# A convolution-attention kernel: layer 1's side projections on two column groups of TensorE, placed behind the sums over the values, and sums of weights used one and a half steps later

## The chip, the cores and the metric

The kernel runs on one core of one Trainium2 chip. The metric is the device time of one execution in microseconds (us), the median of three runs. Everything is computed in fp32.

## The reference

The input is x, two images of 256 channels and 64 x 64 = 4096 positions. Two attention layers follow each other; the second works on the output of the first.

```
layer 0: xn = layernorm over channels(x);  q, k, v = qkv_w xn    (4 heads of 16)
         attn = softmax(q k^T / 4) * gate(x);  x1 = sigmoid(gamma * out_w(attn v) + x)
layer 1: q, k, v = w_qkv x1 + b_qkv                             (4 heads of 64)
         attn = softmax(q k^T / 8) over 4096 positions
         out = w_out(attn v) + b_out + x1
```

The change touches layer 1 alone. There each image has 4 heads of 64 channels, and each head a 4096 x 4096 matrix of scores.

## The kernel before

**How layer 1 is tiled.** Two heads are worked on together: head 0 of a pair on partitions 0 to 63, head 1 on 64 to 127. A *unit* is (image, pair, block of 512 queries): 2 x 2 x 8 = 32 units, one after the other. Within a unit the keys come in 32 chunks of 128. A *step* takes two chunks, so a unit has 16 steps, and the 512 steps run as one long pipeline. In a step, the first chunk is called chunk 0 and the second chunk 1.

For each chunk the following is done:

- score (L876, TensorE): keys times queries, both heads at once on two row groups (64x128 tiles), into a pair of PSUM banks. There are two such pairs, one for each chunk of a step (in the first unit's beginning a third helps).
- keep (L893 and L894): VectorE takes the running maximum rmax over the chunks from the banks; then ScalarE copies the scores to SBUF (raw). The second copy frees the banks.
- 22 chunks (LAG = 11 steps) later, when the maximum of the group of 16 chunks is known: shift (L951, VectorE) adds the negated maximum, weigh (L963, ScalarE) takes the exponential in place, and GpSimd adds the result to a running sum of weights acc (L973 for the first two of a group, then L975).
- gather (L1004, TensorE): values times weights, summed over the 16 chunks of a group in one bank (av), the two heads on two column groups (128x64 tiles). At the end of a group ScalarE copies av out (L1015).

**The order is written out by hand.** Every instruction is kept in program order on its engine (seq). A main loop runs over the steps t and issues, besides the chunk work, whatever was hung at (t, place) by at():

```
scores = [score(c) for c in pair] if inside else []
weigh(pair[1] - 2 * LAG - 2)         # the exponential of the step before
hung(t, "start"); hung(t, "early")
keep(pair[0], scores[0]); shift(pair[0] - 2 * LAG); weigh(pair[0] - 2 * LAG)
hung(t, "early end")
keep(pair[1], scores[1])
for c in pair: gather(c - 2 * LAG - 2)
hung(t, "late"); hung(t, "late end")
shift(pair[1] - 2 * LAG); hung(t, "end")
```

(The loop is shortened; conditions for the first and last steps are left out.) So TensorE's order in a step is: scores of both chunks, what is hung at early, the sums over the values of two chunks, what is hung at late. ScalarE's order is: exponential of the step before, what is hung at start, first copy, exponential, what is hung at early end, second copy.

**What is hung there.** Beside the chunk work, each unit computes things for later units. Counted in steps from the unit's first:

- Keys for the next pair or image: the projection in quarters in steps 2 to 5 (next_keys, quarter, L806), one matmul of 128 channels x 256 positions a step; then store_keys (L818, ScalarE, step 5), and a DMA to DRAM (kd).
- Values: four blocks of 128 positions, each with two matmuls, one block in each of steps 6, 7, 9 and 10 (next_values, values_in, L693); store_values (L832) in steps 7 and 10, the DMA (vd) behind the second.
- Queries of the next unit: quarters in steps 11 (two), 13 and 14 (next_queries); keep_next_queries (L858) in steps 11 and 14. Their input is fetched on SyncE's queue (L656) into three rotating buffers, which the keys' and values' input shares.
- In the last eight units there are no keys and values to make. In their places the first image's output is projected (project_out, L1160) and evacuated (output, L1170).
- The maxima of each group of 16 chunks: turn_max (rt, L906, four transposes) in steps 0 and 8, once early and once late; fold (L923, VectorE, negs), a round trip through DRAM (L926, L930), and place_shift (L943, ScalarE) at the end of steps 2 and 10.
- The sums of weights of the unit before: total (L1026, eight passes on four column groups of 32) in step 12 early; keep_total (L1034, and L1046 for the factor lost) in step 12, with four DMAs to DRAM (L1039) and one back (L1041); add_sums on GpSimd (L1117, L1118) in step 13, late end; factors in step 15, start: the reciprocal on VectorE (L1124) and a product on GpSimd (L1125).
- The output rows of the unit before that: turn_sums (turned, L1051) in step 1, early and late; rows (L1135 on VectorE, L1141 and L1144 on GpSimd), then the store att (L1149).

All small results (k1p, v1p, q1p, o, rt, sum, turned) pass through one PSUM bank (misc, psm with bufs=1): the next one can start only when the one before has been evacuated.

Of the kernel before, what the change touches and what calls it, by code (L numbers as in the profile page):

```python
# [14 lines left out]
P = 128  # L15
NB = 512
C = 256
CC = C // P
H = 4
D0 = 16  # L20
D1 = 64
# [5 lines left out]
def conv_attention_kernel(  # L27
# [19 lines left out]
    nc = tc.nc  # L47
# [78 lines left out]
    for s in range(3):  # L126
        t = const_prep.tile([P, CC, P], F32, tag=f"wpad{s}", name=f"wpad{s}")
# [80 lines left out]
    seq = tc.keep_in_program_order  # L208
# [3 lines left out]
    def at(t, place, step):  # L212
        extras.setdefault((t, place), []).append(step)
# [19 lines left out]
    with own0:  # L233
# [456 lines left out]
        def values_in(ps, xt, g, k):  # L690

            for c in range(CC):
                seq(nc.tensor.matmul(  # L693
                    ps[:, bass.ts(k, P)], xt[:, c, bass.ts(k, P)], w1[:, c, 2, bass.ts(g, P)],
                    start=(c == 0), stop=(c == CC - 1),
                ))
# [71 lines left out]
    with (  # L768
# [31 lines left out]

        def quarter(ps, xt, g, t, q):

            c, cols = q % 2, bass.ts(q // 2, NB // 2)
            seq(nc.tensor.matmul(  # L806
                ps[:, cols], w1[:, c, t, bass.ts(g, P)], xt[:, c, cols],
                start=(c == 0), stop=(c == CC - 1),
            ))

        def next_keys(b, g, i, q):
            if q == 0:
                halves_of["k"] = misc(f"k1p_{b}_{g}_{i}")
            quarter(halves_of["k"], loaded["kv", b, g, i], g, 1, q)

        def store_keys(b, g, i):
            k = l1.tile([P, NB], F32, tag="kv", name=f"k1s_{b}_{g}_{i}")
            seq(nc.scalar.activation(  # L818
                k, halves_of.pop("k"), AF.Identity, bias=b1[:, g, 1:2]
            ))  # L820
            nc.sync.dma_start(out=kd[b, g, i], in_=k)

        def next_values(b, g, i, q):
            if q % 2 == 0:
                halves_of["vp"] = misc(f"v1p_{b}_{g}_{i}_{q}")
            values_in(halves_of["vp"], loaded["kv", b, g, i], g, q)

        def store_values(b, g, i, half):
            if half == 0:
                halves_of["v"] = l1.tile([P, NB], F32, tag="kv", name=f"v1s_{b}_{g}_{i}")  # L830
            v, cols = halves_of["v"], bass.ts(half, NB // 2)
            seq(nc.scalar.copy(v[:, cols], halves_of.pop("vp")[:, cols]))  # L832
            if half == 1:
                loaded.pop(("kv", b, g, i))
                nc.sync.dma_start(out=vd[b, g, i], in_=v)
# [11 lines left out]
        def next_queries(u, q):  # L847
            b, g, j = u
            if q == 0:
                qt = l1x.tile([P, NB], F32, tag="q", name=f"q1_{b}_{g}_{j}")  # L850
                qs1[u] = qt
            if q % 2 == 0:
                halves_of["q"] = misc(f"q1p_{b}_{g}_{j}_{q}")
            quarter(halves_of["q"], loaded["q", u], g, 0, q)

        def keep_next_queries(u, half):
            cols = bass.ts(half, NB // 2)
            seq(nc.scalar.activation(  # L858
                qs1[u][:, cols], halves_of.pop("q")[:, cols], AF.Identity,
                bias=b1[:, u[1], 0:1],  # L860
            ))
            if half == 1:
                loaded.pop(("q", u))
# [154 lines left out]
        def total(u):  # L1018


            b, g, j = u
            srows[u] = misc(f"sum1_{b}_{g}_{j}")
            for n in range(NG):
                for k in range(2):
                    r = D1 * n + 32 * k
                    seq(nc.tensor.matmul(  # L1026
                        srows[u][r : r + 32, :], ones[:, :32], accs[u, n][:, k, :],
                        start=True, stop=True,
                    ))
# [126 lines left out]
        def project_out(b, j, o, q):  # L1156
            if q == 0 or o == 1 and q == 2:
                outs["ps"] = misc(f"o1_{b}_{j}_{o}_{q}")
            c, cols = q % 2, bass.ts(q // 2, NB // 2)
            seq(nc.tensor.matmul(  # L1160
                outs["ps"][:, cols], wo1[:, c, bass.ts(o, P)], loaded["ao", b, j][:, c, cols],
                start=(c == 0), stop=(c == CC - 1),
            ))

        def output(b, j, o, part):

# [23 lines left out]

        for n, u in enumerate(units):
            b, g, j = u
            t0 = n * US
            if n > 0:
                at(t0 - 9, "start", lambda u=u, b=b, j=j: fetch(("q", u), x1[b][j]))
                for q in range(4):
                    at(t0 - (5, 5, 3, 2)[q], "early", lambda u=u, q=q: next_queries(u, q))
                at(t0 - 5, "early end", lambda u=u: keep_next_queries(u, 0))  # L1200
                at(t0 - 2, "early end", lambda u=u: keep_next_queries(u, 1))
            if n < len(units) - NJ:
                to = (*units[n + NJ][:2], j)
                at(max(t0 - 1, 0), "start", lambda to=to: fetch(("kv", *to), x1[to[0]][to[2]]))
                for q in range(4):
                    at(t0 + 2 + q, "early", lambda to=to, q=q: next_keys(*to, q))
                    at(t0 + (6, 7, 9, 10)[q], "early", lambda to=to, q=q: next_values(*to, q))
                at(t0 + 5, "early end", lambda to=to: store_keys(*to))
                for i, step in enumerate((t0 + 7, t0 + 10)):
                    at(step, "early end", lambda to=to, i=i: store_values(*to, i))  # L1210

                t1 = (n // NJ * NJ + NJ - 1) * US
                at(t1 + 2 * j + 2, "start", lambda to=to: load_keys(*to))
                at(t1 + 2 * j + 3 + LAG, "start", lambda to=to: load_values(*to))
            for k in range(NG):
                t1 = t0 + (k + 1) * GS // 2
                places = ("early", "early" if (u, k) == (units[-1], NG - 1) else "late")
                for i, place in enumerate(places):
                    at(t1, place, lambda u=u, k=k, i=i: turn_max(u, k, i))
                    at(t1, f"{place} end", lambda u=u, k=k, i=i: fold(u, k, i))  # L1220
                at(t1 + 2, "end", lambda u=u, k=k: place_shift(u, k))
            t1 = t0 + US + GS // 2
            if u != units[-1]:
                at(t1 + 4, "early", lambda u=u: total(u))
                at(t1 + 4, "early end", lambda u=u: keep_total(u))
                at(t1 + 1, "late", lambda u=u: lose(u))
                at(t1 + 5, "late end", lambda u=u: add_sums(u))
                at(t1 + 7, "start", lambda u=u: factors(u))
                for place, k in (("early", 1), ("late", 0)):
                    at(t1 + 9, place, lambda u=u, k=k: turn_sums(u, k))  # L1230
                    at(t1 + 9, f"{place} end", lambda u=u, k=k: rows(u, k))
            else:
                at(END + 1, "late", lambda u=u: last_lost(u))
                at(END + 4, "early", lambda u=u: late_sums((None, None)))
                at(END + 4, "early end", lambda u=u: keep_late(0))
                at(END + 5, "early", lambda u=u: turn_late(0))
                at(END + 5, "early end", lambda u=u: add_late(u, 0))
                at(END + 6, "early", lambda u=u: turn_sums(u, 0))
                at(END + 6, "early end", lambda u=u: first_rows(u))
                at(END + LAG, "late", lambda u=u: turn_late(1))  # L1240
                at(END + LAG, "late", lambda u=u: add_late(u, 1))
                at(END + LAG, "late", lambda u=u: turn_sums(u, 1))
                at(END + LAG, "late", lambda u=u: last_rows(u))
            if n >= len(units) - NJ:
                b0 = B - 2
                at(t0 - 1, "start", lambda b0=b0, j=j: fetch_output(b0, j))
                for o in range(CC):
                    for q in range(4):
                        step = t0 + ((2, 3, 4, 5), (6, 7, 9, 10))[o][q]
                        at(step, "early", lambda b0=b0, j=j, o=o, q=q: project_out(b0, j, o, q))  # L1250
                at(t0 + 5, "early end", lambda b0=b0, j=j: output(b0, j, 0, 2))
                for part, step in enumerate((t0 + 7, t0 + 10)):
                    at(step, "early end", lambda b0=b0, j=j, part=part: output(b0, j, 1, part))

# [169 lines left out]
```

## Time and profile before

| what | us |
|---|---|
| three runs: median (lowest to highest) | 4672.76 (4672.19 to 4673.68) |
| profiled execution: its own time | 4667.5 |
| profiled execution: span from first to last instruction | 4665.7 |
| first score matmul of layer 1, from the span's start | 2057.6 |
| from one unit's first score matmul to the next one's (units 10 and 11) | 79.80 |
| busy over the span: TensorE / VectorE / ScalarE / GpSimd | 4496.5 / 3894.2 / 3429.5 / 2513.9 |

How to read it: the profile page gives, per engine, the time in which an instruction was under way. TensorE's figure includes waiting inside its pipeline, so a TensorE that is called busy need not be at its peak. Layer 1 is regular: from the second unit on, units follow each other at 78.7 to 80.5 us, so one unit (here unit 10, 2834.7 to 2914.5 us) stands for all. In the timeline a line is: start in us, length in us, engine, line, operation, output<-inputs, shape, number of instructions merged, and in brackets the idle time ahead of it and what ended it. In the list of waits a line is: who <- whom, total us, times, longest us. VectorE's rows overlap a little: an L951 or L893 row is 1.21 us long, and the next one starts 1.13 us after it.

### The profile page before, as it was taken

To read this page: it belongs to the slowest core of one execution; us is meant where nothing else is said; L and a number is where in the kernel's file an instruction comes from. 1 tells how busy PE (TensorE), PEld (TensorE's weight loads), DVE (VectorE), ACT (ScalarE), POOL (GpSimd) and SP (SyncE) were. 2 spreads that over 40 slices of the span, in tenths; PEclk is the share of its full clock that TensorE was granted. 3 is DMA by queue.
4 is the path that set the end of the run, shared out by engine and by line. 5 is a ranking of instruction groups with operands and counts; after the bars stand their busy time and mean duration, and the time that the engine had idled before them with its cause. 6 is when DMAs were issued, how large, how long until landed. Compare 5 with 4: busy or idle time off the path is not lost. (4 is left out here: it accounts for less than half of the span.)

```text
span 4665.7 us, 70910 instructions
## 1 busy us (share of the span) xinstructions
PE 4496.5 (96%) x27290; PEld 1511.0 (32%) x27290; DVE 3894.2 (83%) x4506; ACT 3429.5 (74%) x4588; POOL 2513.9 (54%) x1306
## 2 busy tenths in 40 slices
PE   8999999999999999999999999999999999999998
PEld 3433333333333333332333333333333333222232
DVE  6777777777777777439999999999999999999997
ACT  3366666666666666668888888888888888888885
POOL 5300000000000000009999999999999999999995
PEclk9999999999999999999999999999999999999999
DMA  3100000000000000121111221111211112121213
GB/s 100 39 4 20 20 20 15 15 15 15 15 17 15 15 13 13 40 77 35 35 37 33 63 48 42 35 37 43 69 41 39 37 33 62 48 53 37 53 39 111
DMA packets 199682, 174.70 MB, mean 37 GB/s; under 512 B 121256, under 2 KB 122088, under 8 KB 199344
## 3 DMA queue, kind: packets, MB, share of 16 engines
q1 hardware_dynamic: 197488, 169.58, 13.9%
q8 instruction: 214, 3.51, 0.3%
q14 instruction: 124, 1.02, 0.1%
q10 hardware_dynamic: 1856, 0.59, 0.1%
HBM read 127.65 MB, written 42.48 MB: 36 GB/s over the span
## 5 line engine op out<-in xcount | busy, mean ns | idle before, releaser
L975 POOL TENSOR_TENSOR acc<-acc,raw 128x1024 f32<-128x1024 f32 x883 | 2095.2, 2373 | 82.3 <-ACT raw L963 21.1
L402 DVE TENSOR_REDUCE mx<-a 128x1 f32<-128x512 f32 x2048 | 1314.4, 685 | 449.7 <-PE a L398 448.7
L439 ACT ACTIVATE p<-s 128x512 f32<-128x512 f32 x2048 | 1107.8, 595 | 702.1 <-PE a L398 369.3
L876 PE MATMUL s<-q,k 64*128 64x512 f32 x4096 | 1120.9, 637 | 126.1 <-ACT raw L894 117.9
L951 DVE TENSOR_TENSOR raw<-raw,shift 128x1024 f32<-128x1024 f32 x1024 | 1234.2, 1209 | 3.9 <-ACT shift L943 2.6
L893 DVE TENSOR_TENSOR rmax<-s,rmax 128x1024 f32<-128x1024 f32 x960 | 1168.7, 1217 | 74.4 <-PE s L876 68.3
L436 PE MATMUL s<-q,kT 32*128 32x512 f32 x4096 | 1218.0, 640 | 0.0
L894 ACT COPY raw<-s 128x1024 f32<-128x1024 f32 x1024 | 1034.2, 1010 | 207.3 <-DVE rmax L893 162.0
L963 ACT ACTIVATE raw<-raw 128x1024 f32<-128x1024 f32 x1024 | 1084.8, 1060 | 133.6 <-DVE raw L951 101.2
L398 PE MATMUL a<-kT,q 32*128 32x512 f32 x4096 | 1129.3, 643 | 1.4 <-DVE mx L402 1.3
L1004 PE MATMUL av<-raw,v 128*64 128x512 f32 x4096 | 992.8, 605 | 3.5 <-ACT raw L963 3.4
L451 PE MATMUL av<-p,v 128*32 128x256 f32 (+1 forms) x7904 | 650.1, 399 | 0.6 <-ACT avs L465 0.6
L876 PEld LDWEIGHTS s<-q,k 64*128 64x128 f32 x4096 | 314.6, 185 | 858.5 <-ACT raw L894 600.9
L501 POOL TENSOR_TENSOR f<-f,dyn 128x16 f32<-128x16 f32 x15 | 3.3, 221 | 1027.3 <-DVE f L500 1027.3
L436 PEld LDWEIGHTS s<-q,kT 32*128 32x128 f32 x4096 | 397.2, 183 | 425.8 <-issue 392.6
L451 PEld LDWEIGHTS av<-p,v 128*32 128x32 f32 x7904 | 157.7, 108 | 751.4 <-issue 737.1
L1004 PEld LDWEIGHTS av<-raw,v 128*64 128x64 f32 x4096 | 247.7, 136 | 468.8 <-issue 350.1
L552 POOL TENSOR_SCALAR res<-res 128x1024 f32<-128x1024 f32 x16 | 16.7, 1045 | 659.6 <-ACT res L551 659.6
L398 PEld LDWEIGHTS a<-kT,q 32*128 32x128 f32 x4096 | 305.1, 183 | 31.5 <-DVE mx L402 18.2
L973 POOL TENSOR_TENSOR acc<-raw,raw 128x1024 f32<-128x1024 f32 x64 | 152.6, 2385 | 124.2 <-ACT raw L963 124.2
L923 DVE TENSOR_REDUCE negs<-rt 128x4 f32<-128x512 f32 x126 | 86.7, 688 | 50.4 <-PE rt L906 50.4
L306 DVE RECIPROCAL std<-std 128x128 f32<-128x128 f32 x64 | 56.1, 920 | 39.5 <-ACT std L301 39.5
(335 smaller groups left out, 1835.1 us busy)
## 6 DMA issues: line engine op xcount, KB each, us to landing
row<-neg SPq DMA_DIRECT2D x128, 256.0 KB
x<-in_x_dram SPq DMA_DIRECT2D x16, 512.0 KB
res<-in_x_dram SPq DMA_DIRECT2D x16, 512.0 KB
x<-res SPq DMA_DIRECT2D x16, 512.0 KB
att<-rows SPq DMA_DIRECT2D x62, 128.0 KB
kd<-k1s SPq DMA_DIRECT2D x24, 256.0 KB
vd<-v1s SPq DMA_DIRECT2D x24, 256.0 KB
k<-kd SPq DMA_DIRECT2D x24, 256.0 KB
```

What stands on the lines that cost most here:

```text
L398: seq(nc.tensor.matmul(ps, qs0[u][r, bass.ts(i, P)], kTs[b][r, bass.ts(m, NB)], start=True, stop=True,))
L402: seq(nc.vector.tensor_reduce(mxs[u][:, i * H + h, m : m + 1], ps, AX.X, ALU.max))
L436: seq(nc.tensor.matmul(ps, kTs[b][r, bass.ts(m, P)], qs0[u][r, :], start=True, stop=True))
L439: seq(nc.scalar.activation(pt[:, k, :], ps, AF.Exp, scale=D0**-0.5))
L451: seq(nc.tensor.matmul(avs[u][32 * h : 32 * h + 32, cols], vs0[b][:, m, 32 * h : 32 * h + 32], pts[t, h // 2][:, h % 2, cols], start=(m == ...
L876: seq(nc.tensor.matmul(ps[:, k, :], ks[b, g, m // PB][r, bass.ts(m % PB, P)], qs1[u][r, :], start=True, stop=True,))
L893: seq(nc.vector.tensor_tensor(rmax[u, n], ps, before, ALU.max))
L894: seq(nc.scalar.copy(raw, ps))
L951: seq(nc.vector.tensor_tensor(raws[t], raws[t], shifts[u, t % NM // GS], ALU.add))
L963: seq(nc.scalar.activation(p, p, AF.Exp, scale=D1**-0.5))
L975: seq(nc.gpsimd.tensor_tensor(accs[u, n], accs[u, n], p, ALU.add))
L1004: seq(nc.tensor.matmul(avs1[u, n][k * D1 : (k + 1) * D1, :], v[:, m % PB, k, :], raws[t][:, k, :], start=(m % GS == 0), stop=(m % GS == GS ...
```

## The change

- quarter issues two matmuls in place of one: output channels 0 to 63 and 64 to 127, each on its own column group of TensorE (128x64 tiles), with half the weights each and the same 256 columns streamed. Keys, queries and the first image's output use it.
- next_values likewise splits each matmul by positions: 64 positions of the input as weights per column group, the same 128 columns of w1 streamed.
- These projections, and total, move from early to late in the same step: from between the scores and the sums over the values to behind those sums.
- Their evacuations on ScalarE, with the DMAs behind them, move from early end of a step to start of the next: keys from step 5 to 6, values from 7 and 10 to 8 and 11, queries from 11 and 14 to 12 and 15, output as keys and values, keep_total from 12 to 13.
- add_sums moves from step 13 late end to step 15 late end; factors from step 15 start to step 0 end.

```diff
--- before.py
+++ after.py
@@ -800,18 +800,20 @@
-        def quarter(ps, xt, g, t, q):
+        def quarter(ps, xt, w, q):
             c, cols = q % 2, bass.ts(q // 2, NB // 2)
-            seq(nc.tensor.matmul(
-                ps[:, cols], w1[:, c, t, bass.ts(g, P)], xt[:, c, cols],
-                start=(c == 0), stop=(c == CC - 1),
-            ))
+            for k in range(2):
+                r = slice(k * D1, (k + 1) * D1)
+                seq(nc.tensor.matmul(
+                    ps[r, cols], w[:, c, r], xt[:, c, cols], start=(c == 0), stop=(c == CC - 1),
+                ))
         def next_keys(b, g, i, q):
             if q == 0:
                 halves_of["k"] = misc(f"k1p_{b}_{g}_{i}")
-            quarter(halves_of["k"], loaded["kv", b, g, i], g, 1, q)
+            quarter(halves_of["k"], loaded["kv", b, g, i], w1[:, :, 1, bass.ts(g, P)], q)
         def store_keys(b, g, i):
             k = l1.tile([P, NB], F32, tag="kv", name=f"k1s_{b}_{g}_{i}")
@@ -823,7 +825,14 @@
         def next_values(b, g, i, q):
             if q % 2 == 0:
                 halves_of["vp"] = misc(f"v1p_{b}_{g}_{i}_{q}")
-            values_in(halves_of["vp"], loaded["kv", b, g, i], g, q)
+            ps, xt = halves_of["vp"], loaded["kv", b, g, i]
+            for c in range(CC):
+                for k in range(2):
+                    r = slice(k * D1, (k + 1) * D1)
+                    seq(nc.tensor.matmul(
+                        ps[r, bass.ts(q, P)], xt[:, c, q * P + k * D1 : q * P + (k + 1) * D1],
+                        w1[:, c, 2, bass.ts(g, P)], start=(c == 0), stop=(c == CC - 1),
+                    ))
         def store_values(b, g, i, half):
             if half == 0:
@@ -851,7 +860,7 @@
                 qs1[u] = qt
             if q % 2 == 0:
                 halves_of["q"] = misc(f"q1p_{b}_{g}_{j}_{q}")
-            quarter(halves_of["q"], loaded["q", u], g, 0, q)
+            quarter(halves_of["q"], loaded["q", u], w1[:, :, 0, bass.ts(g, P)], q)
         def keep_next_queries(u, half):
             cols = bass.ts(half, NB // 2)
@@ -1156,11 +1165,7 @@
         def project_out(b, j, o, q):
             if q == 0 or o == 1 and q == 2:
                 outs["ps"] = misc(f"o1_{b}_{j}_{o}_{q}")
-            c, cols = q % 2, bass.ts(q // 2, NB // 2)
-            seq(nc.tensor.matmul(
-                outs["ps"][:, cols], wo1[:, c, bass.ts(o, P)], loaded["ao", b, j][:, c, cols],
-                start=(c == 0), stop=(c == CC - 1),
-            ))
+            quarter(outs["ps"], loaded["ao", b, j], wo1[:, :, bass.ts(o, P)], q)
         def output(b, j, o, part):
@@ -1190,24 +1195,25 @@
         for n, u in enumerate(units):
             b, g, j = u
             t0 = n * US
             if n > 0:
                 at(t0 - 9, "start", lambda u=u, b=b, j=j: fetch(("q", u), x1[b][j]))
                 for q in range(4):
-                    at(t0 - (5, 5, 3, 2)[q], "early", lambda u=u, q=q: next_queries(u, q))
-                at(t0 - 5, "early end", lambda u=u: keep_next_queries(u, 0))
-                at(t0 - 2, "early end", lambda u=u: keep_next_queries(u, 1))
+                    at(t0 - (5, 5, 3, 2)[q], "late", lambda u=u, q=q: next_queries(u, q))
+                at(t0 - 4, "start", lambda u=u: keep_next_queries(u, 0))
+                at(t0 - 1, "start", lambda u=u: keep_next_queries(u, 1))
             if n < len(units) - NJ:
                 to = (*units[n + NJ][:2], j)
                 at(max(t0 - 1, 0), "start", lambda to=to: fetch(("kv", *to), x1[to[0]][to[2]]))
                 for q in range(4):
-                    at(t0 + 2 + q, "early", lambda to=to, q=q: next_keys(*to, q))
-                    at(t0 + (6, 7, 9, 10)[q], "early", lambda to=to, q=q: next_values(*to, q))
-                at(t0 + 5, "early end", lambda to=to: store_keys(*to))
-                for i, step in enumerate((t0 + 7, t0 + 10)):
-                    at(step, "early end", lambda to=to, i=i: store_values(*to, i))
+                    at(t0 + 2 + q, "late", lambda to=to, q=q: next_keys(*to, q))
+                    at(t0 + (6, 7, 9, 10)[q], "late", lambda to=to, q=q: next_values(*to, q))
+                at(t0 + 6, "start", lambda to=to: store_keys(*to))
+                for i, step in enumerate((t0 + 8, t0 + 11)):
+                    at(step, "start", lambda to=to, i=i: store_values(*to, i))
                 t1 = (n // NJ * NJ + NJ - 1) * US
                 at(t1 + 2 * j + 2, "start", lambda to=to: load_keys(*to))
@@ -1221,11 +1227,11 @@
                 at(t1 + 2, "end", lambda u=u, k=k: place_shift(u, k))
             t1 = t0 + US + GS // 2
             if u != units[-1]:
-                at(t1 + 4, "early", lambda u=u: total(u))
-                at(t1 + 4, "early end", lambda u=u: keep_total(u))
+                at(t1 + 4, "late", lambda u=u: total(u))
+                at(t1 + 5, "start", lambda u=u: keep_total(u))
                 at(t1 + 1, "late", lambda u=u: lose(u))
-                at(t1 + 5, "late end", lambda u=u: add_sums(u))
-                at(t1 + 7, "start", lambda u=u: factors(u))
+                at(t1 + 7, "late end", lambda u=u: add_sums(u))
+                at(t1 + 8, "end", lambda u=u: factors(u))
                 for place, k in (("early", 1), ("late", 0)):
                     at(t1 + 9, place, lambda u=u, k=k: turn_sums(u, k))
                     at(t1 + 9, f"{place} end", lambda u=u, k=k: rows(u, k))
@@ -1247,10 +1253,10 @@
                 for o in range(CC):
                     for q in range(4):
                         step = t0 + ((2, 3, 4, 5), (6, 7, 9, 10))[o][q]
-                        at(step, "early", lambda b0=b0, j=j, o=o, q=q: project_out(b0, j, o, q))
-                at(t0 + 5, "early end", lambda b0=b0, j=j: output(b0, j, 0, 2))
-                for part, step in enumerate((t0 + 7, t0 + 10)):
-                    at(step, "early end", lambda b0=b0, j=j, part=part: output(b0, j, 1, part))
+                        at(step, "late", lambda b0=b0, j=j, o=o, q=q: project_out(b0, j, o, q))
+                at(t0 + 6, "start", lambda b0=b0, j=j: output(b0, j, 0, 2))
+                for part, step in enumerate((t0 + 8, t0 + 11)):
+                    at(step, "start", lambda b0=b0, j=j, part=part: output(b0, j, 1, part))
```

## The prediction

> **What bounds the kernel now.** I read the page first: the engines' shares and the 40 slices show layer 1 (from about 2057 us on) with TensorE, VectorE and GpSimd all at 9 tenths. Then the busy time over one unit of 16 steps (unit 10: its first score matmul is at 2834.71, that of unit 11 at 2914.51), then who waited for whom in that unit, then its timeline.
>
> ```profile
> 2834.70:2914.50 79.80, 75.74 (x322) 24.78 (x320) 75.97 (x71) 69.51 (x76) 74.20 (x37) 1.00 0.16 37
> ```
>
> The columns after the length are PE, PEld, DVE, ACT and POOL, then the granted clock (1.00), the DMA share and GB/s. DVE, the busiest, is idle for 79.80 - 75.97 = 3.83 us a unit. The successive units start 79.8 us apart, so what a unit loses is worth some 31 times as much.
>
> ```profile
> ACT raw L894 <- DVE rmax L893: 4.8, 8, 0.8
> ...
> PE s L876 <- ACT raw L894: 3.4, 7, 0.8
> ...
> POOL acc L973 <- ACT raw L963: 2.9, 2, 2.1
> ...
> DVE rmax L893 <- PE s L876: 2.1, 5, 0.6
> DVE negs L923 <- PE rt L906: 1.6, 3, 0.6
> ```
>
> The waits form a ring: DVE's maximum waits for the scores, ACT's copy for the maximum, the next scores for the copy that frees their pair of banks. DVE's idle time is almost all behind PE: 2.1 us for scores and 1.6 us for turned maxima. POOL has 3.5 us to spare. The timeline of steps 5 to 7 shows such a wait arise:
>
> ```profile
> 2865.74 0.67 ACT L818 ACTIVATE k1s<-k1p,b 128x512 f32<-128x512 f32 x1
> ...
> 2866.31 1.00 ACT L894 COPY raw<-s 128x1024 f32<-128x1024 f32 x1
> ...
> 2867.36 1.13 PE L876 MATMUL s<-q,k 64*128 64x512 f32 x4 [0.56 <-ACT raw L894]
> ...
> 2868.42 0.71 PE L693 MATMUL v1p<-w,xb_('kv', 1, 0, 2)_23934 128*128 128x128 f32 x4
> ...
> 2869.06 1.94 PE L1004 MATMUL av<-raw,v 128*64 128x512 f32 x8
> ...
> 2870.93 1.99 PE L876 MATMUL s<-q,k 64*128 64x512 f32 x8
> ...
> 2872.11 1.22 DVE L893 TENSOR_TENSOR rmax<-s,rmax 128x1024 f32<-128x1024 f32 x1 [0.58 <-PE s L876]
> ```
>
> The store of the keys (L818) holds up the copy, the copy holds up the second scores, PE then runs without a pause through v1p, av and the next scores, and DVE stands 0.58 us.
>
> **What the skill says.** TensorEngine Tiling (Array Packing), Key Properties: changing the tiling mode drains TensorE. The trace agrees: second scores to projection takes 1.06 us, projection to av 0.64, av to scores 1.87; where nothing lies between (step 15) scores to av takes 1.06 and av to scores 1.87. The passes of av start 0.43 us apart (weight loads at 2863.80, 2864.28, 2864.71) for 512 columns, so the 2 passes of 256 (keys) or 4 of 128 (values) need 0.43; the other 0.2 of 0.64 is the extra change of mode. PSUM — Partial Sum Buffer, PSUM bank collisions: two engines must be kept apart on one bank even if both read; the copy indeed starts 0.08 us after the maximum ends. TensorE: Matmul & The Clock Gate, Architectural detail (queue depths): ACT and DVE are strict FIFO, so each inserted instruction delays everything behind it; L818 above does that.
>
> **The change, part by part** (per unit).
>
> *Two column groups behind av.* av runs in 128x64 tiles; so will keys, values, queries and output. Order becomes scores, av, projection, scores: two mode changes instead of three. Streaming stays 0.43 if the two 64-wide halves run at once, as av's do (1.94 us for eight passes, pairs at the same time). Saved on PE: 0.2 in each of 11 steps (4 keys, 4 values, 3 with queries) = 2.2 us. The trace doesn't show two groups that stream the same columns: at best 0.43, at worst one after the other, 0.86, which is 0.23 more than the 0.63 of today per quarter. I take 0.43, since av's two streams already run side by side.
>
> *av earlier in its step.* It meets its second exponential sooner: that ends 1.2 us after the second scores start, av's second half is needed 1.06 + 0.9 = 1.97 after, cover 0.8. In steps 3 and 11 the copy of shifts (L943, 1.04 us) delays the exponential: a stall of about 0.2 there, which eats that step's gain.
>
> *ACT stores from before the second copy to before the first of the next step.* The first copy feeds scores with more than 1 us to spare (2868.23 to 2869.24, used at 2870.93), and ACT has 0.13 us free at each operation behind DVE, three times until the second copy: it absorbs 0.39. So k1s (0.57) delays a second copy by 0.18 in place of 0.34; v1s (0.25), queries (0.35) and sums with lost (0.61) by nothing to 0.2.
>
> *A new wait.* Maxima are turned in step 8 in the same single bank (misc) as the first half of the values, whose store now stands in step 8 behind an exponential: 2876.75 + 0.96 + 0.36 + 0.08 = 2878.15, against rt's start at 2877.84. PE stands 0.31, and with it av, the second rt and the second fold (wait 0.27 today). The first fold has DVE work as cover. In step 0 the queries' store is a step earlier: no wait.
>
> *Sums of weights.* total goes behind av: 128x32 tiles either way, three mode changes before and after, so nothing. Its sums' five DMAs leave SP a half-step later, about 2904 in place of 2901; they were read at 2908.3 without a wait, and will be after 2914: hidden behind accumulations, 8 us of cover. On SP only the fetch of 2908.68 stands behind them. The reciprocal (0.27) moves from step 15 to the end of step 0; the POOL product behind it finds POOL busy until 8.9 us into the unit and the reciprocal done at 7.9: cover 1 us, afterwards POOL and rows would wait one for one.
>
> *Other queues.* SP fetches the next queries' input when the last values are computed (issued 2889.15, used 2892.97); both move back by the same av, so the 3.8 us remain. The stores to kd, vd and out go 1 to 3 us later with nothing on SP due before step 8 or 13. POOL's work is unchanged: 30 accumulations at 2.45, and 3.3 for the rest = 76.8 a unit, the floor.
>
> DVE's idle time by place, today and after: folds of step 0, 1.28 and 1.28 (behind a copy that DVE sets). Steps 4 and 5, 0.44 and 0.24 (0.2 of PE). Step 7, 0.58 less 0.34 (k1s gone) less 0.2 = 0.04, and 0.19 at step 8 for the displaced k1s. Step 8's fold, 0.27 and 0.58. Step 11, 0.25 and 0.05. Step 12, 0.36 and 0.15 (the savings of steps 10 and 11, less step 11's stall). Step 13, 0.57 and 0.50: from the second maximum of step 11 it is 1.31 to the copy, 1.05 to the scores, 3.92 with av and total to the next scores, 1.18 to their maximum, 7.46, of which DVE's six operations fill 6 x 1.133 = 6.8 and step 12's wait 0.15; total saves nothing. Reciprocal, 0.08 and 0.08. Sum: 3.83 today, as measured, and 3.11 after. Gain 0.72 us x 31 = 22 us. The profiled execution took 4667.5 (span 4665.7), 5.3 under the median of 4672.76; 22 us off gives 4645 in it, and 4650 at the median.
>
> **Rivals.** (a) *All of PE's saving arrives.* 2.2 x 31 = 68 us: about 4605. For it: the ring runs through PE wherever DVE waits, and one shortened step helps the next. Against: POOL's floor leaves 3.0 a unit at most, and DVE has only 2.1 behind scores. (b) *No change:* the wait moves to rt and to ACT's displaced stores; if k1s and v1s cost DVE their full 0.57 and 0.25, 0.63 more than counted, 0.09 a unit is left, 3 us: 4670. For it: ACT's gaps are only 0.13 each. Against: there are three of them ahead of each second copy. (c) *Slower:* the two halves don't overlap. Each quarter then costs 0.86 on PE behind av, 12 quarters x 0.23 = 2.8 us a unit more than today, half of it on the path, as an estimate, since DVE waits for PE in about half of the steps: 31 x 1.4 = 43, 4716. It decides from 0.63 a quarter on. For it: the halves read the same columns, which no row here shows; against: av. (d) *The change doesn't do what it says:* if the projections still changed mode, their place alone would bring the step's order but no PE time; that is counted with (b).
>
> **How the numbers follow.** Forecast (gain 10 to 40) 0.58; (a), over 40, 0.14; (b) with (d), within 9 us, 0.15; (c) or a like loss, 0.13. 0.2% (9 us) is what a measurement of this kernel can tell from no change. Faster 0.72, same 0.15, slower 0.13. The range reaches up over (b), to 4674, and down to 4615, half of (a)'s cases; outside lie (c) at 0.11 and the rest of (a) at 0.08.
>
> **What would show it.** Right: av directly after the scores 1.06 us later, a projection 0.43 to 0.5 behind it, units 79.1 apart, DVE's wait for scores 1.2 instead of 2.1, and a new wait of rt for v1s of 0.3. Wrong: projections over 0.63 (c), rt waiting over 1 us, POOL or rows waiting for the reciprocal, PE's queries for their DMA.

## The result, and the profile after

| | us (runs) | ratio to before, 95% interval |
|---|---|---|
| before | 4673.58 (4672.19 to 4674.93, 6) | |
| after | 4654.17 (4653.08 to 4655.26, 6) | 0.9959 [0.9949, 0.9969] |

The forecast was 4650, in a range of 4615 to 4674. In the views PE is TensorE (PEld its weight loads), DVE is VectorE, ACT is ScalarE and POOL is GpSimd. The profiled execution of after took 4653.08 (span 4651.2). Its place among the runs differs from that of before: the profiled execution of before lay 6 us under the median, that of after 1 us under. So the two spans differ by 14.5 us only, and the medians by 19.4; why is not known. Where the working below is held against the traces, 14.5 is the figure; the experiments are compared by their ratios.

One unit of after, the same unit 10, again as length, PE, PEld, DVE, ACT, POOL, clock, DMA share and GB/s:

```profile
2831.44:2910.60 79.16, 74.59 (x354) 24.35 (x353) 75.92 (x71) 69.84 (x76) 74.24 (x37) 1.00 0.16 37
```

The unit is 0.64 us shorter. DVE has the same 71 instructions and the same busy time (75.92, 75.97 before), so the whole gain is idle time that DVE lost: 79.16 - 75.92 = 3.24 in place of 3.83. Over units 4 to 30 the mean went from 79.88 to 79.30. The waits in this unit:

```profile
PE s L885 <- ACT raw L903: 3.6, 8, 0.8
...
ACT raw L903 <- DVE rmax L902: 2.8, 5, 0.8
...
POOL acc L982 <- ACT raw L972: 2.7, 2, 2.0
...
DVE negs L932 <- PE rt L915: 1.8, 3, 0.6
...
DVE rmax L902 <- PE s L885: 1.0, 2, 0.6
...
PE rt L915 <- ACT v1s L841: 0.2, 1, 0.2
```

Line numbers have moved by nine (L893 is now L902, L906 is L915). Waits of 0.14 us and less are not in this list; DVE has a few of them, and they stand in the table by place further down. DVE's wait for scores fell from 2.1 us in five places to 1.0 in two, its wait for turned maxima rose from 1.6 to 1.8, and the last line is new: the first transposes of step 8 wait for the bank that holds the values. Steps 5 to 7 of after, the stretch that was shown of before:

```profile
2864.59 0.67 ACT L820 ACTIVATE k1s<-k1p,b 128x512 f32<-128x512 f32 x1
...
2864.68 1.94 PE L1013 MATMUL av<-raw,v 128*64 128x512 f32 x8
...
2865.16 1.00 ACT L903 COPY raw<-s 128x1024 f32<-128x1024 f32 x1
...
2866.44 0.61 PE L832 MATMUL v1p<-w,xb_('kv', 1, 0, 2)_24089 128*64 128x128 f32 x8
...
2866.98 2.29 PE L885 MATMUL s<-q,k 64*128 64x512 f32 x8
...
2867.07 1.01 ACT L903 COPY raw<-s 128x1024 f32<-128x1024 f32 x1
...
2868.16 1.22 DVE L902 TENSOR_TENSOR rmax<-s,rmax 128x1024 f32<-128x1024 f32 x1
...
2869.20 1.94 PE L1013 MATMUL av<-raw,v 128*64 128x512 f32 x8
```

The projection v1p now stands between av and the next scores and takes 0.54 us from start to start (2866.44 to 2866.98); av ahead of it takes 1.77 (from 2864.68; the rounded starts give 1.76). The store of the keys stands ahead of a first copy (2865.16), the second copy comes at 2867.07, and the maximum at 2868.16 has no bracket: of DVE's 0.58 us at this place 0.04 is left.

### The profile page after: what moved, and what is told of

Read it like the earlier page. It is cut to its first block, busy times and chain, and to the rows that moved or that the text cites. A ratio compares the mean times of both kernels' runs of the same rounds, so it can differ in the third digit from the quotient of the medians.

```text
span 4651.2 us, 72702 instructions
## 1 busy us (share of the span) xinstructions
PE 4461.5 (96%) x28242; PEld 1497.3 (32%) x28242; DVE 3894.5 (84%) x4506; ACT 3439.9 (74%) x4588; POOL 2515.1 (54%) x1306
## 5 line engine op out<-in xcount | busy, mean ns | idle before, releaser
L902 DVE TENSOR_TENSOR rmax<-s,rmax 128x1024 f32<-128x1024 f32 x960 | 1169.5, 1218 | 48.3 <-PE s L885 37.3
L1013 PE MATMUL av<-raw,v 128*64 128x512 f32 x4096 | 1014.2, 608 | 10.0 <-ACT raw L972 6.5
L915 PE MATMUL rt<-ident,rmax 128*128 128x128 f32 x504 | 82.7, 287 | 9.3 <-ACT v1s L841 5.7
```

The costliest lines, as they stand in the source:

```text
L902: seq(nc.vector.tensor_tensor(rmax[u, n], ps, before, ALU.max))
L1013: seq(nc.tensor.matmul(avs1[u, n][k * D1 : (k + 1) * D1, :], v[:, m % PB, k, :], raws[t][:, k, :], start=(m % GS == 0), stop=(m % GS == GS ...
```

## The experiments

All kernels below compute everything that the reference asks for. Each ratio is to the kernel before on the same chip. "DVE idle" is unit 10's length less DVE's busy time, "unit" the mean of units 4 to 30.

| kernel | ratio | unit | DVE idle |
|---|---|---|---|
| before | | 79.88 | 3.83 |
| after | 0.9959 [0.9949, 0.9969] | 79.30 | 3.24 |
| e1 groups, old places | 0.9966 [0.9953, 0.9978] | 79.35 | 3.41 |
| e2 whole matmuls, new places | 0.9998 [0.9990, 1.0006] | 79.82 | 3.69 |
| e3 sums moved alone | 1.0004 [0.9996, 1.0012] | 79.96 | 3.91 |
| e4 after, values stored earlier | 0.9936 [0.9924, 0.9949] | 78.92 | 2.91 |
| e5 e4, queries spread | 0.9927 [0.9914, 0.9939] | 78.73 | 2.69 |
| e6 e4, projections early | 1.0050 [1.0037, 1.0063] | 80.65 | 4.79 |
| e7 after, sums at old places | 1.0009 [1.0001, 1.0017] | 79.97 | 4.04 |
| e8 e1, sums moved | 0.9966 [0.9952, 0.9979] | 79.32 | 3.49 |
| e9 e5, whole matmuls | 0.9981 [0.9973, 0.9989] | 79.52 | 3.35 |

My theory: the saved change of tiling mode (the tile shape in which TensorE works) carries the gain, and the new places only move waits. The rival: the new places carry it (av earlier, ACT's stores out of the way of the second copy), and the groups are by the way.

### e1 and e2: groups alone, places alone

e1 is the kernel before with the new quarter and next_values (the diff's first four hunks), every at() as before. e2 is the reverse:

```diff
-                    at(t0 + 2 + q, "early", lambda to=to, q=q: next_keys(*to, q))
...
+                    at(t0 + 2 + q, "late", lambda to=to, q=q: next_keys(*to, q))
...
```

and all other at() lines as in after, with one 128x128 matmul a quarter.

> The column groups alone: projections and evacuations stay where they were before the change (projections between the scores and av). Mode theory (the gain is the third change of tiling mode, saved wherever the projection stands beside av): projection to av 0.43 to 0.45 us instead of 0.64, units of 79.1 to 79.3 instead of 79.8, 4650 to 4658 with the kernel before at 4673. Place theory (the gain comes from av standing directly behind the scores and from evacuations ahead of the first copy): units of 79.8, 4673.

> The places alone: projections as whole 128x128 matmuls, but behind av, evacuations and sums as in the changed kernel. Mode theory: three changes of mode as before, so TensorE saves nothing; what the displaced stores give back (0.3 at the keys, 0.35 at the queries) is about lost again where rt waits for the values' store; 4665 to 4676. Place theory: as the changed kernel, 4654.

Measured: e1 0.9966, e2 0.9998. The groups give 0.0034 without the places; the places as they stand in after give nothing without the groups. So the rival fell. That the places give nothing is a balance, though. From e1 to after DVE's gap in step 7 of unit 10 falls from 0.38 to 0.04 and the one in step 13 from 0.77 to 0.47, but the second fold's rises from 0.27 to 0.56 and step 12's from 0.34 to 0.57. e4 and e5 below take up the two that rose. TensorE's timeline in e1 (a step with keys, in the old order) and then in e2 shows why:

```profile
2849.96 0.65 PE L809 MATMUL k1p<-xb_('kv', 1, 0, 2)_24094,w 128*64 128x256 f32 x4
2850.44 1.89 PE L1013 MATMUL av<-raw,v 128*64 128x512 f32 x8
2852.26 0.70 PE L885 MATMUL s<-q,k 64*128 64x512 f32 x2
```

```profile
2857.10 0.70 PE L806 MATMUL k1p<-xb_('kv', 1, 0, 2)_23929,w 128*128 128x256 f32 x2
2857.73 2.25 PE L876 MATMUL s<-q,k 64*128 64x512 f32 x8
2859.92 1.94 PE L1004 MATMUL av<-raw,v 128*64 128x512 f32 x8
```

Read the starts, not the lengths. In e1 a projection costs 0.48 to the start of av (0.43 to 0.45 was expected), in e2 0.63 to the scores. From the second scores of a step to the first of the next (start to start, where PE waits for nothing), in order of issue:

| kernel | order after the second scores | intervals | sum |
|---|---|---|---|
| before | projection, av, scores | 1.06, 0.64, 1.87 | 3.57 |
| e2 | av, projection, scores | 1.06, 1.87, 0.63 | 3.56 |
| e1 | projection, av, scores | 1.06, 0.48, 1.82 | 3.36 |
| after | av, projection, scores | 1.06, 1.77, 0.53 | 3.36 |

For TensorE the order does not count; the mode does, 0.20 to 0.21 us a step. A step without a projection (step 15) takes 1.06 and 1.87, 2.93 in all, before and after. So a projection adds 0.43 in av's mode, and 0.63 to 0.64 outside it.

Could the whole matmuls be slower for another reason, their width? Step 11 of before, which has two whole quarters one behind the other, says no:

```profile
2892.97 1.13 PE L806 MATMUL q1p<-b_('q', (0, 1, 3))_24164,w 128*128 128x256 f32 x4
...
2894.03 1.94 PE L1004 MATMUL av<-raw,v 128*64 128x512 f32 x8
```

The two take 1.06 from start to start and one takes 0.63, so the second whole quarter adds 0.43. In after, two quarters of halves take 0.96 and one 0.53 (lines under e5): the second adds 0.43 too. Width for width they cost the same; the 0.2 is paid once for each group of whole matmuls, at its two ends.

### e3, e7 and e8: the sums of weights

e3 is the kernel before with the sums' four moves alone, e8 the same on e1, e7 is after with them undone:

```diff
-                at(t1 + 4, "late", lambda u=u: total(u))
-                at(t1 + 5, "start", lambda u=u: keep_total(u))
+                at(t1 + 4, "early", lambda u=u: total(u))
+                at(t1 + 4, "early end", lambda u=u: keep_total(u))
...
-                at(t1 + 7, "late end", lambda u=u: add_sums(u))
-                at(t1 + 8, "end", lambda u=u: factors(u))
+                at(t1 + 5, "late end", lambda u=u: add_sums(u))
+                at(t1 + 7, "start", lambda u=u: factors(u))
```

> The kernel before with only the sums of weights moved: total behind av, its evacuation in the next step, add_sums two steps and the factors one and a half steps later. Mode and place theories alike: within 4 us of the kernel before, since total needs as many changes of mode in either place. If the sums carry the gain: 4654.

> The changed kernel with total, its store, add_sums and factors at their old places (step 12 early, step 12 early end, step 13, step 15). By the theory that the move of the sums is made necessary by the queries' new place: total needs the misc bank in step 12 before the sums over the values, and the queries' store now stands at the start of step 12 behind an exponential; PE waits some 0.6 us for it, 0.5 a unit is lost, 15 us, ratio near 0.999. If the sums' place is indifferent here as it was alone in the old kernel (1.0004): 0.9959.

> Column groups, projections and their stores at the places of the kernel before, but the sums of weights at the places of the changed kernel. It asks whether the sums' new place gives anything of its own once the mode changes are gone, and it parts e1 (0.9966, all old places) from the changed kernel (0.9959, all new places). If the sums' place matters only through the queries' store, as the run with the old sums in the changed kernel suggests (13 us lost there): 0.9966 within 0.001 here. If the sums' new place is a gain of its own, which the old kernel hid behind other waits: below 0.9955. DVE's gap of 0.77 in step 13 of e1, which has total behind the scores, is where it would show.

Measured: e3 1.0004 and e8 0.9966, so alone and on the groups the move gives nothing. e7 is 1.0009 against after's 0.9959: without the move, 0.0050 or some 23 us would have been lost, more than the whole gain. (The 13 us named in e8's expectation are a slip; it was 23.) The timeline of e7's step 12 shows where:

```profile
2898.75 0.50 ACT L867 ACTIVATE q<-q1p,b 128x256 f32<-128x256 f32 x1
...
2899.39 1.06 PE L1035 MATMUL sum<-acc,ones 128*32 128x512 f32 x8 [0.77 <-ACT q L867]
...
2903.43 1.22 DVE L902 TENSOR_TENSOR rmax<-s,rmax 128x1024 f32<-128x1024 f32 x1 [1.31 <-PE s L885]
```

The queries' store has moved from step 11 to the start of step 12, behind an exponential; total at its old place wants the same misc bank and stands 0.77 us, with av and the next scores behind it, and DVE stands 1.31 in step 13 (after: 0.47). So the sums' move is not a gain; it is what the later stores require. Expected were some 15 us for 0.6; the wait was 0.77, and DVE's gap grew by 0.84.

### e4: the values' first store half a step earlier

```diff
-                for i, step in enumerate((t0 + 8, t0 + 11)):
-                    at(step, "start", lambda to=to, i=i: store_values(*to, i))
+                for i, at_ in enumerate(((t0 + 7, "end"), (t0 + 11, "start"))):
+                    at(*at_, lambda to=to, i=i: store_values(*to, i))
```

and the same for the first image's output. The store comes ahead of the second exponential of step 7 in place of behind it.

> The changed kernel with the first half of the values (and of the second output block) evacuated at the end of step 7, ahead of the exponential, instead of the start of step 8. If the wait of rt for v1s is a real cost: rt starts 0.25 us earlier, the second fold's wait falls from 0.56 to about 0.3, units of 78.9, 4646. If ScalarE's delay comes back at the next score instead: units of 79.16, 4654.

Measured: 0.9936, better than after by 0.0023 (11 us). First step 8 of after, then the same place in e4:

```profile
2873.77 0.35 ACT L841 COPY v1s<-v1p 128x256 f32<-128x256 f32 x1
...
2874.18 0.66 PE L915 MATMUL rt<-ident,rmax 128*128 128x128 f32 x4 [0.25 <-ACT v1s L841]
...
2877.32 0.69 DVE L932 TENSOR_REDUCE negs<-rt 128x4 f32<-128x512 f32 x1 [0.56 <-PE rt L915]
```

```profile
2868.22 0.38 ACT L841 COPY v1s<-v1p 128x256 f32<-128x256 f32 x1
...
2869.43 0.66 PE L915 MATMUL rt<-ident,rmax 128*128 128x128 f32 x4
...
2872.59 0.69 DVE L932 TENSOR_REDUCE negs<-rt 128x4 f32<-128x512 f32 x1 [0.24 <-PE rt L915]
```

The bank is free 0.8 us before the transposes want it, the wait is gone, and the second fold waits 0.24 in place of 0.56. The new wait that the prediction priced at 0.31 was real, and cost its size. With it gone e4 is also ahead of e1 (0.9966), and the two intervals do not touch: the new places do give something to the groups, once this wait no longer takes it back.

### e5: what makes DVE stand in step 12

This was my largest miss: 0.15 forecast, 0.57 measured. Steps 10 to 12 of after:

```profile
2888.22 1.11 ACT L952 COPY shift<-row 128x1024 f32<-128x1024 f32 x1
...
2889.28 2.18 PE L1013 MATMUL av<-raw,v 128*64 128x512 f32 x8
...
2891.29 1.03 PE L809 MATMUL q1p<-b_('q', (0, 1, 3))_24330,w 128*64 128x256 f32 x8
...
2892.25 1.86 PE L885 MATMUL s<-q,k 64*128 64x512 f32 x6
...
2893.43 1.22 DVE L902 TENSOR_TENSOR rmax<-s,rmax 128x1024 f32<-128x1024 f32 x1 [0.57 <-PE s L885]
```

The copy of shifts delays the exponential that av's second half needs (av: 2.18 in place of 1.94, about 0.2 late), and two query quarters follow (0.96 from start to start, a single one 0.53). In e4 the gap is 0.57 as well. e5 takes e4 and puts one quarter a step later:

```diff
-                    at(t0 - (5, 5, 3, 2)[q], "late", lambda u=u, q=q: next_queries(u, q))
-                at(t0 - 4, "start", lambda u=u: keep_next_queries(u, 0))
+                    at(t0 - (5, 4, 2, 2)[q], "late", lambda u=u, q=q: next_queries(u, q))
+                at(t0 - 3, "start", lambda u=u: keep_next_queries(u, 0))
...
-                at(t1 + 4, "late", lambda u=u: total(u))
-                at(t1 + 5, "start", lambda u=u: keep_total(u))
+                at(t1 + 5, "late", lambda u=u: total(u))
+                at(t1 + 6, "start", lambda u=u: keep_total(u))
```

> The version with the values' first store at the end of step 7, and in addition the queries' quarters spread out: steps 11, 12 and two in 14 (instead of two in 11, one in 13, one in 14); their first store moves to the start of step 13, total to step 13 late, its store to step 14. It asks what makes DVE stand 0.57 in step 12, where 0.15 was forecast. If it is the double quarter behind the stalled av of step 11 (0.96 in place of 0.53): the gap of step 12 falls to about 0.3, that of step 13 to about 0, one of 0.5 to 0.6 shows in step 14, where two quarters and total's late effect now stand; idle DVE time about 0.2 less a unit, 31 x 0.2 = 6 us, ratio near 0.992. If the stall comes from the copy of shifts and the exponential alone: step 12 stays at 0.57 and the ratio is that of the version with the early store, 0.9936.

Measured: 0.9927. The gap of step 12 fell from 0.57 to 0.14:

```profile
2884.63 0.60 PE L809 MATMUL q1p<-b_('q', (0, 1, 3))_24330,w 128*64 128x256 f32 x4
...
2885.16 1.13 PE L885 MATMUL s<-q,k 64*128 64x512 f32 x4
...
2886.34 1.23 DVE L902 TENSOR_TENSOR rmax<-s,rmax 128x1024 f32<-128x1024 f32 x1
```

It fell by 0.43, which is 0.96 - 0.53, the one quarter moved. So the double quarter behind the stalled av made the gap, and the shift copy alone does not. I had the size in step 12 too small (0.3) and the place of the rest wrong: 0.32 is left in step 13 (expected about 0), 0.19 each in steps 14 and 15 (expected 0.5 to 0.6 and 0). The sum over steps 12 to 15 went from 1.07 to 0.84, 0.23 a unit, as expected. Against e4 the intervals overlap; the verdict on step 12 rests on the trace, not on the time. e5 is the fastest version of the study, 4632.58 us on its chip (before there 4667.18).

### e6: early projections with late stores

```diff
-                    at(t0 + 2 + q, "late", lambda to=to, q=q: next_keys(*to, q))
-                    at(t0 + (6, 7, 9, 10)[q], "late", lambda to=to, q=q: next_values(*to, q))
+                    at(t0 + 2 + q, "early", lambda to=to, q=q: next_keys(*to, q))
+                    at(t0 + (6, 7, 9, 10)[q], "early", lambda to=to, q=q: next_values(*to, q))
```

with queries and output alike, all on e4.

> The version with the values' first store at the end of step 7, but with the projections back between the scores and the sums over the values (sums of weights and evacuations stay as in that version). By the theory of mode changes the place is indifferent: projection and av are in one mode, so two changes a step either way; 0.9936 within 0.001. By the theory that av's earlier place feeds the ring, the ratio moves back by over 0.001 toward 0.9966, that of the groups alone in the old places.

Measured: 1.0050, far outside both. The experiment was badly cut: it changed two things. Its list of waits tells what I had overlooked:

```profile
DVE rmax L902 <- PE s L885: 3.2, 5, 1.7
...
PE q1p L809 <- ACT v1s L841: 1.3, 1, 1.3
...
PE v1p L832 <- ACT k1s L820: 0.6, 1, 0.6
...
PE q1p L809 <- ACT srow L1043: 0.5, 1, 0.5
```

With the store at the start of the next step, the first projection of the next result must stand behind av, or it meets a bank that is still full. So its time says nothing on the place alone, and no other run moves the projections with nothing else moved. For TensorE's own time its trace agrees with the table above: where TensorE waits for nothing, a step with keys or values takes 3.36 us in e6 too. What e6 does say is that late stores need late projections. The same mechanism is in after, where no av lies between: in unit 0, whose first sums over the values come only in step 12, TensorE's waits of after hold

```profile
PE q1p L809 <- ACT v1s L841: 0.9, 1, 0.9
PE v1p L832 <- ACT k1s L820: 0.8, 1, 0.8
```

Before has neither. Steps 6 and 11 of unit 0 are longer by 0.85 and 0.91, 0.7 of it is made up, and unit 0 takes 61.0 in place of 59.9.

### e9: the mode change under the better schedule

e9 is e5 with one 128x128 matmul a quarter, as e2 was to after.

> The schedule of the fastest version (values' first store at the end of step 7, queries' quarters in steps 11, 12, 14, 14), but with the whole 128x128 matmuls of the kernel before. It measures the value of the mode change under a second schedule: between e2 (0.9998) and the changed kernel (0.9959) it was 0.0039, 18 us. If the mode change is the cause, and DVE waits for PE in the same places: 0.9927 + 0.004 = 0.997, with 0.10 us more at each projection and units 0.6 us longer. If the schedule alone makes the fast version: 0.993.

Measured: 0.9981, against e5's 0.9927. The groups are worth 0.0034 in the old places (e1), 0.0039 in the new (after against e2), 0.0054 in e5's: 16, 18 and 25 us. I expected 0.004 here. The schedule alone gives 0.0019. So the two do add, and in e5's schedule more of the same saving arrived than in the other two: the units differ by 0.53, 0.52 and 0.79 us for the same eleven steps with projections.

## Why the prediction was right, and where it was wrong

**Right in sign and mechanism.** Faster by 0.41% [0.31, 0.51], where 4650 meant 0.49% of the runs shown then. *The bound*: DVE's idle time behind PE was what could be gained, and nothing else moved: DVE's busy time is the same to 0.05 us. *The mode change*: 0.2 a step was counted, 0.20 to 0.21 measured. The Trainium skill, TensorEngine Tiling (Array Packing), Key Properties, states that a changed mode drains the engine, on which the forecast leaned, and that different tiles can run in parallel, which the forecast took from av's rows alone. The traces agree with both. The four half-width passes of a quarter, which stream the same columns in pairs, take 0.48 ahead of av and 0.53 behind it, where two whole passes took 0.63 to 0.64; rival (c), the halves one after the other, would have shown 0.86 and is out. The projections do run in av's mode, which rules out (d); and the measured 19.4 us, with an interval of about 14 to 24, lies clear of (a) with 68 and of (b) with 3.

**Also right.** The stall of av's second half in steps 3 and 11 (about 0.2 forecast; the half starts 1.10 us behind the first in place of 0.91). The reciprocal and its product with 1 us of cover: at 2839.10 and 2840.44, and nothing waits for them. The wait of the transposes: 0.31 forecast, 0.25 measured. Sums of weights: nothing by themselves, as e3 and e8 show; that they had to move because the queries' store did, the prediction did not see.

DVE's idle time by place, forecast and measured in unit 10 of after:

| place | forecast | measured |
|---|---|---|
| folds of step 0 | 1.28 | 1.28 |
| steps 3 to 5 (called 4 and 5) | 0.24 | 0.04 + 0.14 + 0.06 |
| step 7 | 0.04 | 0.04 |
| step 8, displaced k1s | 0.19 | 0 |
| step 8, second fold | 0.58 | 0.56 |
| step 11 | 0.05 | 0.04 |
| step 12 | 0.15 | 0.57 |
| step 13 | 0.50 | 0.47 |
| step 15 (called reciprocal) | 0.08 | 0.04 |
| sum | 3.11 | 3.24 |

Two rows need a word. The 0.44 that the prediction read for steps 4 and 5 of before holds 0.04 of step 3, behind the copy of shifts. And the reciprocal has left step 15; the 0.04 there is a wait for scores, and where the reciprocal stands now DVE loses nothing.

**Step 12, the term that failed.** The prediction took today's 0.36 and subtracted "the savings of steps 10 and 11, less step 11's stall". Savings don't add up across steps once PE waits for DVE. In after PE stands between the two score groups of step 11 (1.16 us from one to the next, 0.99 in before), because the copy behind DVE's maximum frees its banks; whatever PE saved before that is gone. The path had to be walked from there, as the prediction did for step 13: from the second maximum of step 10, 1.31 to its copy, 1.07 to the second scores of step 11, 1.06 to av, 1.10 to its delayed second half, 0.91 to the two quarters, 0.96 to the scores of step 12, 1.18 to their maximum, 7.59 in all. DVE's six operations and a short gap fill 7.02 (from 54.40 to 61.42 us into the unit), and 0.57 remain. In before the same path took 7.56, of which DVE filled 7.20. So the path got no shorter: step 11's stall ate what its change of mode saved (av's halves and the two quarters take 2.97 together, 2.93 before), and step 10's saving does not lie on it. DVE, whose own gap in step 11 had shrunk from 0.25 to 0.04, only came to the wait earlier. Step 13, which was walked, came out at 0.47 for 0.50.

**Step 8, a size.** The displaced store of keys was to delay a second copy by 0.57 - 3 x 0.13 = 0.18. It delayed it by nothing. ACT's slack is not the idle time between its rows: an exponential is 1.06 us long, but the next copy can start 0.96 after its start, and the exponential behind a copy 0.89 (smallest spacings seen), while behind DVE the spacings are 1.19 and 1.07. From the exponential at 2863.62 to the second copy at 2867.07 it is 3.45 us with the store in between, and 1.19 + 1.07 + 1.19 = 3.45 without one. The three spacings at their smallest take 0.96 + 0.89 + 0.96 = 2.81, so the slack was 0.64, not 0.39, and the store's 0.57 fits in.

**The total.** Forecast 22 us (31 x 0.72), measured 14.5 between the two profiled executions: units 1 to 30 give 16.6 (0.55 each on the mean), unit 0 loses 1.1 to the bank (e6's mechanism), which the prediction did not look at, and from unit 31 on the span is 1.0 longer (154.2 for 153.2), whose cause was not tried; e4 (152.9) and e7 (153.0) do not have it.

## What to carry to other kernels

Give small matmuls the tile shape of their neighbour on TensorE: here half-width pairs in av's mode stream in the same time and save a change of mode, and on which side of av they stood made no difference to TensorE's time (3.36 us either way). What such a move does to the waits is another matter: as first made it gave nothing that the runs could tell (0.9966 and 0.9959), and with one store moved again it did (0.9936). When work moves later, follow what it holds: each store put half a step later held the one small PSUM bank longer, and three users of it (transposes, total, the next projection) either waited or had to move as well. And forecast a wait by walking the path from the last operation of the bounding engine, not by subtracting savings from today's wait.

## What the runs showed of the hardware

- A change of mode shows at the ends of a group of matmuls, not inside it. av alone takes 1.87 to the scores and 1.77 to a projection in its own mode: 0.10 for the change behind it. A whole 128x128 projection between groups of other modes takes 0.63 to 0.64 to what follows, in either order (before, e2), and a second one behind it adds only 0.43: 0.20 for its two ends, in a step that then has three changes in place of two.
- 128x32 tiles count as another mode than 128x64: av to total takes 1.87, as av to scores does.
- ACT's rows of 128x1024 overlap: the copy is 1.01 long and the exponential 1.06, but the smallest spacings seen from start to start are 0.89 and 0.96.
